# One sample of a streaming kernel is loaded as two halves, the second on four DMA engines

## Chip, core and metric

The kernel runs on one core of a Trainium2 chip. The metric is device time in microseconds (us), as the median of several executions. Times inside an execution come from one execution taken by the hardware profiler; they are counted from the start of its span, which is a little shorter than the execution's own time.

## What is computed

`x` is 128 samples of 128 x 1024 floats (512 KB each, 64 MB in all), `weights` holds eight 128 x 128 matrices, and `subjects` (the input `itok_B_0_7`) gives each sample the number of its matrix. Every sample is multiplied by its own matrix and added to the product:

```
B, C, D, T, N_SUBJECTS = (128, 128, 128, 1024, 8)
w = weights[subjects]
out = jnp.einsum('bct,bcd->bdt', x, w)
return x + out
```

All of `x` has to be read from HBM and all of the result, another 64 MB, written back.

## The kernel before

The samples go through in 32 groups of four (G = 2 samples in a pair, H = 2 pairs in a group, `NT` = 32). A group `i` lives in one of 12 SBUF slots, `xs[i % 12]`, each 128 partitions x 4 samples x 1024 floats. The result overwrites the sample in its slot and is stored from there.

Four sequences run side by side and meet in semaphores:

- **SP issues all loads**, in order of the samples (the loop at line 162). Each load is one DMA of 512 KB with a completion of 16 on the semaphore of its pair, `s_pair[slot][pair]`. Its HBM side is written as 32 rows of 16 KB (`ROWS` = 4 rows of `x` put together), its SBUF side as 128 partitions of 4 KB; spread over 16 DMA engines this is two pieces of 16 KB for each engine. The first 48 loads fill the 12 slots without a wait; from group 12 on, SP first waits until the store that empties the slot has landed (lines 164 to 167).
- **POOL copies the matrix** of each sample from `w_all` to one of four small buffers (line 196). Ahead of the first copy of a pair it waits that the PSUM buffer is free (`s_added`), and the copy itself carries the wait for the two loads of its pair (`loaded(i, q0)`).
- **PE and DVE** follow: two matmuls of 512 columns for each sample (line 206), then one addition over the pair (line 217).
- **ACT issues the stores**, one of 2 MB for each group, smaller ones for the first and the last group. The very last sample has a store of its own at line 231.

The semaphore arithmetic matters for the change: `s_pair` counts 16 for each load of the pair and 16 for the store of the group, and `loaded` and `emptied` give the counts to wait for. The function `transfer` (line 50) builds the DMA instruction with its access patterns as they are written, so the shapes of the two sides reach the queue unmerged.

Of the kernel before, what the change touches and what calls it, by code (L numbers as in the profile page):

```python
# [30 lines left out]
G = 2  # L31
H = 2
# [3 lines left out]
SLOTS = 12  # L36
# [5 lines left out]
DMA = 16  # L42

IDLE = 3

ROWS = 4
QUEUES = {mybir.EngineType.SP: "qSPDynamicHW", mybir.EngineType.Activation: "qActDynamicHW"}


def transfer(nc, engine, out, in_):  # L50

    later, nc._always_lower_symbolic_ap = nc._always_lower_symbolic_ap, False
    ins, outs = engine.lower_ap_dma(in_), engine.lower_ap_dma(out)
    nc._always_lower_symbolic_ap = later
    return engine.add_instruction(  # L57
        mybir.InstDMACopy(
            name=nc.get_next_instruction_name(),
            engine=engine.engine,  # L60
            ins=ins,
            outs=outs,
            mode="Copy",
            cce_op=ALU.bypass,
            queue=QUEUES[engine.engine],
        )
    )


@with_exitstack  # L70
def kernel(
    ctx: ExitStack,
    tc: tile.TileContext,
    x: bass.AP,
    subjects: bass.AP,
    weights: bass.AP,
    out: bass.AP,
):
    nc = tc.nc
    B, C, T = x.shape  # L80
    S, _, D = weights.shape
    NT = B // (G * H)

    def sbuf(name, *shape, dtype=F32):
        return ctx.enter_context(nc.sbuf_tensor(name, list(shape), dtype)).ap()

    given, near, wrap, index = (
        sbuf(name, 1, B, dtype=I32) for name in ("given", "near", "wrap", "index")
    )
    w_all = sbuf("w_all", C, S, D)  # L90
    ws = [sbuf(f"w{i}", C, 1, D) for i in range(W_SLOTS)]
    zeros = sbuf("zeros", C, N)
    xs = [sbuf(f"x{i}", C, H * G, T) for i in range(SLOTS)]
    ps = [
        ctx.enter_context(nc.psum_tensor(f"ps{i}", [D, G, T], F32)).ap() for i in range(P_SLOTS)
    ]

    s_given = tc.alloc_semaphore("s_given")
    s_wall = tc.alloc_semaphore("s_wall")
    s_index = tc.alloc_semaphore("s_index")  # L100
    s_zeros = tc.alloc_semaphore("s_zeros")
    s_copied = tc.alloc_semaphore("s_copied")
    s_product = tc.alloc_semaphore("s_product")
    s_added = tc.alloc_semaphore("s_added")

    s_pair = [[tc.alloc_semaphore(f"s_pair{i}_{h}") for h in range(H)] for i in range(SLOTS)]


    s_first = tc.alloc_semaphore("s_first")

    def emptied(i, h):

        turns = i // SLOTS
        return (DMA * G + (DMA if h == H - 1 else 0)) * turns

    def loaded(i, q):

        h = q // G
        return s_pair[i % SLOTS][h], emptied(i, h) + DMA * G

    def load(engine, i, q):
        k, h = i % SLOTS, q // G
        transfer(
            nc,
            engine,
            xs[k][:, q, :],
            x[i * H * G + q].rearrange("(a r) t -> a (r t)", r=ROWS),
        ).then_inc(s_pair[k][h], DMA)

    def store(i, q0, q1):  # L130
        k, b = i % SLOTS, i * H * G
        transfer(
            nc,
            nc.scalar,
            out[b + q0 : b + q1].rearrange("g d t -> d g t"),
            xs[k][:, q0:q1, :].rearrange("d (o g) t -> d o (g t)", g=min(G, q1 - q0)),
        ).then_inc(s_first if i == 0 and q1 == G else s_pair[k][(q1 - 1) // G], DMA)

    with tc.tile_critical():  # L139

        nc.scalar.dma_start(given, subjects.rearrange("(o b) -> o b", o=1)).then_inc(s_given, DMA)

        nc.vector.memset(zeros, 0.0).then_inc(s_zeros, 1)  # L143
        nc.tensor.wait_ge(s_zeros, 1)
        for _ in range(IDLE):
            nc.tensor.matmul(  # L146
                ps[P_SLOTS - 1][:, G - 1, :N], zeros[:, :D], zeros, start=True, stop=True
            )

        nc.vector.wait_ge(s_given, DMA)
        nc.vector.tensor_scalar(near, given, -S, S - 1, ALU.max, ALU.min).then_inc(s_index, 1)  # L153
        nc.vector.wait_ge(s_index, 1)
        nc.vector.tensor_scalar(wrap, near, 0, S, ALU.is_lt, ALU.mult).then_inc(s_index, 1)  # L155
        nc.vector.wait_ge(s_index, 2)
        nc.vector.tensor_tensor(index, near, wrap, ALU.add).then_inc(s_index, 1)  # L157
        nc.gpsimd.wait_ge(s_index, 3)


        nc.sync.dma_start(w_all, weights.rearrange("s c d -> c s d")).then_inc(s_wall, DMA)  # L161
        for i in range(NT):
            k = i % SLOTS
            if i == SLOTS:
                nc.sync.wait_ge(s_first, DMA)
            if i >= SLOTS:
                nc.sync.wait_ge(s_pair[k][H - 1], emptied(i, H - 1))
            for q in range(H * G):
                load(nc.sync, i, q)


        for j in range(NT * H):
            i, q0, q1 = j // H, j % H * G, (j % H + 1) * G
            k = i % SLOTS
            p = ps[j % P_SLOTS]

            ahead = j < P_SLOTS
            if ahead:  # L180
                nc.tensor.wait_ge(*loaded(i, q0))
            for q in range(q0, q1):
                b = i * H * G + q
                if b % R == 0:
                    _, subject = nc.values_load_multi_w_load_instructions(
                        index[0:1, b : b + R],
                        engines=[mybir.EngineType.Pool],
                        min_val=0,
                        max_val=S - 1,
                        skip_runtime_bounds_check_because="the index is clamped on the chip above",  # L190
                    )
                if b == 0:
                    nc.gpsimd.wait_ge(s_wall, DMA)
                if not ahead and q == q0:
                    nc.gpsimd.wait_ge(s_added, j - P_SLOTS + 1)
                copy = nc.gpsimd.tensor_copy(  # L196
                    ws[b % W_SLOTS], w_all[:, bass.ds(subject[b % R], 1), :]
                )
                if not ahead and q == q0:
                    copy.wait_op(*loaded(i, q0), "sem-ge")  # L200
            copy.then_inc(s_copied, 1)

            nc.tensor.wait_ge(s_copied, j + 1)
            for q in range(q0, q1):
                for t in range(0, T, N):
                    mm = nc.tensor.matmul(  # L206
                        p[:, q % G, t : t + N],
                        ws[(i * H * G + q) % W_SLOTS][:, 0, :],
                        xs[k][:, q, t : t + N],
                        start=True,  # L210
                        stop=True,
                    )
            mm.then_inc(s_product, 1)

            mine = xs[k][:, q0:q1, :]
            nc.vector.wait_ge(s_product, j + 1)
            nc.vector.tensor_tensor(  # L217
                mine, p, mine, ALU.add
            ).then_inc(s_added, 1)

            if i == 0 or q1 == H * G or i == NT - 1:
                nc.scalar.wait_ge(s_added, j + 1)
                store(i, q0 if i in (0, NT - 1) else 0, q1 - (b == B - 1))

    with tc.tile_critical() as waits:
        for i in range(NT - SLOTS, NT):
            nc.sync.wait_ge(s_pair[i % SLOTS][H - 1], emptied(i + SLOTS, H - 1))
        nc.sync.wait_ge(s_pair[(NT - 1) % SLOTS][0], emptied(NT - 1 + SLOTS, 0) + DMA)  # L230
    last = nc.scalar.dma_start(out[B - 1], xs[(NT - 1) % SLOTS][:, H * G - 1, :])

    tc.add_manual_dep(
        last.ins,
        waits.name,
        mybir.DependencyInfo(mybir.DependencyClass.NoSync, mybir.DependencyReason.SCHED_ONLY),
        reason="the end of the program waits for it",
    )
# [27 lines left out]
```

## Time and profile before

| what | value |
|---|---|
| median of 3 runs | 326.78 us (326.64 to 326.98) |
| the profiled execution | 327.18 us |
| its span | 325.4 us |
| data moved | 134.85 MB: 67.63 MB read from HBM, 67.11 MB written |
| packets of the loads' queue (q1, issued by SP) | 7184 |
| packets of the stores' queue (q10, issued by ACT) | 8882 |
| last matmuls and last addition end | 278.7 us |
| last store issued | 305.0 us |
| granted TensorE clock, mean | 0.924 |

How to read it: the compute engines are done some 46 us before the end. What is left in that time are stores that had been queued. The profile counts the share of time that the core's 16 DMA engines were moving packets; a share of 0.06 is one engine of 16. A few packets are neither loads nor stores: eight in the span are instruction fetches (four of 16 KB on queue q8, four of 8 KB on q14).

A DMA's completion is posted in 16 parts, one by each DMA engine after its own last piece. The trace has the time of each posting, though not the number of the engine.

### The profile page before, as it was taken

To read this page: it belongs to the slowest core of one execution; us is meant where nothing else is said; L and a number is where in the kernel's file an instruction comes from. 1 tells how busy PE (TensorE), PEld (TensorE's weight loads), DVE (VectorE), ACT (ScalarE), POOL (GpSimd) and SP (SyncE) were. 2 spreads that over 40 slices of the span, in tenths; PEclk is the share of its full clock that TensorE was granted. 3 is DMA by queue.
4 is the path that set the end of the run, shared out by engine and by line. 5 is a ranking of instruction groups with operands and counts; after the bars stand their busy time and mean duration, and the time that the engine had idled before them with its cause. 6 is when DMAs were issued, how large, how long until landed. Compare 5 with 4: busy or idle time off the path is not lost.

```text
span 325.4 us, 1606 instructions
## 1 busy us (share of the span) xinstructions
PE 241.1 (74%) x518; PEld 95.2 (29%) x518; DVE 147.9 (45%) x68; POOL 34.3 (11%) x132
## 2 busy tenths in 40 slices
PE   6999988988888888888888888888888689000000
PEld 2444332333333333333333333333333233000000
DVE  1375754555555555454555555554554544200000
POOL 1011111011111111111011111111111010000000
PEclk9999999999999999999999999999999889655555
DMA  6999999999999999999999999999999999999994
GB/s 250 413 418 421 428 425 422 420 428 427 426 421 427 429 415 427 424 431 423 423 435 417 416 432 424 428 417 428 433 419 424 418 437 415 429 425 427 426 428 201
DMA packets 16074, 134.85 MB, mean 414 GB/s; under 512 B 2625, under 2 KB 3650, under 8 KB 3906
## 3 DMA queue, kind: packets, MB, share of 16 engines
q1 hardware_dynamic: 7184, 67.64, 49.7%
q10 hardware_dynamic: 8882, 67.11, 49.1%
q8 instruction: 4, 0.07, 0.1%
q14 instruction: 4, 0.03, 0.0%
HBM read 67.63 MB, written 67.11 MB: 414 GB/s over the span
## 4 chain that ended last, share of the span: by engine, by line
PE 42%; DVE 20%; issue 16%; POOL 4%; DMA 2%; POOLq 1%; SPq 0%
PE ps L206 42%; DVE x L217 20%; POOL w L196 4%; DMA x<-in_x_dram 2%; POOLq L196 1%; SPq L57 0%; SPq L161 0%; POOLq L139 0%; SPq L262 0%; SPq L139 0%
## 5 line engine op out<-in xcount | busy, mean ns | idle before, releaser
L206 PE MATMUL ps<-x,w 128*128 128x512 f32 x512 | 236.1, 607 | 33.6 <-POOL w L196 32.1
L217 DVE TENSOR_TENSOR x<-ps,x 128x2048 f32<-128x2048 f32 x64 | 146.7, 2292 | 129.1 <-PE ps L206 129.1
L206 PEld LDWEIGHTS ps<-x,w 128*128 128x128 f32 x512 | 93.3, 191 | 176.6 <-issue 93.9
L196 POOL COPY w<-w_all 128x128 f32 x128 | 34.1, 296 | 238.0 <-DMA x<-in_x_dram 207.7
L146 PE MATMUL ps<-zeros 128*128 128x512 f32 x6 | 5.0, 992 | 1.7 <-DVE zeros L143 1.7
L146 PEld LDWEIGHTS ps<-zeros 128*128 128x128 f32 x6 | 1.8, 328 | 3.7 <-issue 2.1
L143 DVE MEMSET zeros<- 128x512 f32 x1 | 0.5, 485 | 1.1 <-SPq L139 1.1
L153 DVE TENSOR_SCALAR near<-given 1x128 int32<-1x128 int32 x1 | 0.2, 215 | 0.6 <-DMA given<-in_itok_B_dram 0.6
L157 DVE CUSTOM_DVE_ANT_0 index<-near,wrap 1x256 uint16<-1x256 uint16 x1 | 0.3, 278 | 0.0
L155 DVE TENSOR_SCALAR wrap<-near 1x128 int32<-1x128 int32 x1 | 0.2, 216 | 0.0
L253 POOL MEMSET const-float32-0.0<- 128x1 f32 x1 | 0.1, 99 | 0.2 <-issue 0.2
L253 POOL MEMSET const-bfloat16-1.0<- 128x1 bf16 x1 | 0.1, 102 | 0.0
L253 POOL MEMSET const-uint8-127<- 128x1 uint8 x1 | 0.1, 102 | 0.0
L253 POOL MEMSET const-float32-1.0<- 128x1 f32 x1 | 0.1, 99 | 0.0
## 6 DMA issues: line engine op xcount, KB each, us to landing
x<-in_x_dram SPq DMA_DIRECT2D x128, 512.0 KB, 32.3
out_dram<-x ACTq DMA_DIRECT2D x30, 2048.0 KB, 47.3
out_dram<-x ACTq DMA_DIRECT2D x3, 1024.0 KB, 13.9
out_dram<-x ACTq DMA_DIRECT2D x2, 512.0 KB, 21.1
w_all<-in_L_cond_weights_dram SPq DMA_DIRECT2D x1, 512.0 KB, 4.5
given<-in_itok_B_dram ACTq DMA_DIRECT2D x1, 0.5 KB
```

The costliest lines, as they stand in the source:

```text
L143: nc.vector.memset(zeros, 0.0).then_inc(s_zeros, 1)
L146: nc.tensor.matmul(ps[P_SLOTS - 1][:, G - 1, :N], zeros[:, :D], zeros, start=True, stop=True)
L153: nc.vector.tensor_scalar(near, given, -S, S - 1, ALU.max, ALU.min).then_inc(s_index, 1)
L155: nc.vector.tensor_scalar(wrap, near, 0, S, ALU.is_lt, ALU.mult).then_inc(s_index, 1)
L157: nc.vector.tensor_tensor(index, near, wrap, ALU.add).then_inc(s_index, 1)
L196: copy = nc.gpsimd.tensor_copy(ws[b % W_SLOTS], w_all[:, bass.ds(subject[b % R], 1), :])
L206: mm = nc.tensor.matmul(p[:, q % G, t : t + N], ws[(i * H * G + q) % W_SLOTS][:, 0, :], xs[k][:, q, t : t + N], start=True, stop=True,)
L217: nc.vector.tensor_tensor(mine, p, mine, ALU.add).then_inc(s_added, 1)
L253: nc = _bacc.Bacc("TRN2", target_bir_lowering=False, num_devices=1)
```

## The change

Sample 40 of 0 to 127 (the 41st; the first of group 10, in slot 10) is loaded by `load_apart` instead of `load`. Partitions 0 to 63 come in one DMA of 16 rows of 16 KB, one row for each of 16 engines, and count on a new semaphore `s_apart`. Partitions 64 to 127 come in a second DMA. Its HBM side is written with an outermost dimension of 4, each with 4 rows of 16 KB; it counts on the pair's semaphore, as the whole load did. By the change's own description these are four pieces for each of the first four engines. POOL waits for `s_apart` ahead of the copy for this sample.

The engines' instruction orders differ in nothing else: SP's 41st load is two DMA instructions in place of one, and POOL has one more wait.

```diff
+APART = 40
+FEW = 4
...
+    s_apart = tc.alloc_semaphore("s_apart")
...
+    def load_apart(engine, i, q):
+
+        k, h = i % SLOTS, q // G
+        half = C // 2
+        rows = x[i * H * G + q]
+        transfer(
+            nc,
+            engine,
+            xs[k][:half, q, :],
+            rows[:half].rearrange("(a r) t -> a (r t)", r=ROWS),
+        ).then_inc(s_apart, DMA)
+        transfer(
+            nc,
+            engine,
+            xs[k][half:, q : q + 1, :],
+            rows[half:].rearrange("(e a r) t -> e a (r t)", r=ROWS, e=FEW),
+        ).then_inc(s_pair[k][h], DMA)
...
             for q in range(H * G):
-                load(nc.sync, i, q)
+                (load_apart if i * H * G + q == APART else load)(nc.sync, i, q)
...
+                if b == APART:
+                    nc.gpsimd.wait_ge(s_apart, DMA)
                 copy = nc.gpsimd.tensor_copy(
```

## The prediction

> **What bounds the kernel now.** I read the DMA parts of the page first, because the compute engines end long before the span does. Rows of the page:
>
> ```profile
> DMA  6999999999999999999999999999999999999994
> ...
> q1 hardware_dynamic: 7184, 67.64, 49.7%
> q10 hardware_dynamic: 8882, 67.11, 49.1%
> q8 instruction: 4, 0.07, 0.1%
> q14 instruction: 4, 0.03, 0.0%
> ```
>
> Loads and stores together fill 98.8% of the time of 16 DMA engines: 321.5 of 325.4 us. The missing 3.9 us are the first two (nothing issued yet), the last one (nothing left), and the stretch in which the engines stop one after the other. The view of windows shows a middle stretch and that end; columns: window, length, busy time of four engines, PE clock, DMA share, GB/s:
>
> ```profile
> 60.00:120.00 60.00, 52.62 (x114) 20.12 (x112) 32.19 (x15) 7.89 (x30) 1.00 1.01 425
> ...
> 275.00:318.00 43.00, 1.35 (x4) 0.28 (x2) 2.29 (x1) 0.00 (x0) 0.55 1.01 426
> 320.00:320.50 0.50, 0.00 (x0) 0.00 (x0) 0.00 (x0) 0.00 (x0) 0.50 0.96 393
> 320.50:321.00 0.50, 0.00 (x0) 0.00 (x0) 0.00 (x0) 0.00 (x0) 0.50 0.57 229
> 321.00:321.50 0.50, 0.00 (x0) 0.00 (x0) 0.00 (x0) 0.00 (x0) 0.50 0.42 172
> 321.50:322.00 0.50, 0.00 (x0) 0.00 (x0) 0.00 (x0) 0.00 (x0) 0.50 0.30 123
> 322.00:323.00 1.00, 0.00 (x0) 0.00 (x0) 0.00 (x0) 0.00 (x0) 0.50 0.06 25
> 323.00:324.00 1.00, 0.00 (x0) 0.00 (x0) 0.00 (x0) 0.00 (x0) 0.50 0.06 25
> ```
>
> The reader is to see three things. All 16 engines are busy until 320.5 us. Then they drop out in a group (0.96 to 0.42) and a second group (0.30 to 0.06). From 322 to 324 us one engine of 16 works alone, at 25 GB/s, about what it had among 16 (425 / 16 = 26.6). So an engine has a pace of its own, and the kernel ends when the engine with most left to do ends. The trace's postings for the very last store say the same to 0.01 us; relative to the last of the 16:
>
> ```
> -3.78 -3.57 -3.48 -3.42 -3.37 -3.32 -3.29 -3.24 -3.03
> -2.39 -2.36 -2.19 -2.15 -2.13 -1.87
>  0.00
> ```
>
> Nine engines end 3.0 to 3.8 us early, six 1.9 to 2.4, and one is the laggard. The eight instruction fetches explain the six: one costs its engine 0.6 to 1.5 us. The laggard got one as well, but most of its lag grows evenly from 22 to 272 us, while loads run; in the store-only tail its packets take 311 ns, as the others' do.
>
> **What the change does to the sum.** From the windows' row, 16,384 B at 26.6 GB/s is 0.617 us for a piece; the pieces' own records say 0.616, and each starts 4 ns before its predecessor ends: 0.61 us. Before, each engine had two pieces of sample 40. After, engines outside the first four have one, the first four 1 + 4 = 5.
>
> - Twelve engines: 1 piece less, -0.61 us.
> - First four: 3 pieces more, 3 x 0.61 = +1.84 us, and one more posting (a 4 B packet of 9 ns).
>
> The bytes stay the same. What decides is where in the list of postings the first four stand, which the trace does not tell, as it gives no engine's number. The bounds are these. If the laggard is outside the four, it ends 0.61 us earlier. The four end at their old place + 1.84: engines of the nine at -3.03 + 1.84 = -1.19 or earlier, never last; engines of the six at -2.39 + 1.84 = -0.55 up to -1.87 + 1.84 = -0.03. So the end moves by -0.61 to -0.03. If the laggard is one of the four, it moves by +1.84.
>
> I take the laggard as outside. Counted over 16 engines the chance is 12 in 16. A row speaks for more: in the load-only stage (8 to 18 us) the 16 postings of each load come in one fixed order within 0.73 us, with one engine 0.12 us ahead of the rest, and the laggard at or next to the end of that order. If pieces are handed out by engine number, the laggard has a high one. Of the six, four would be spread over 15 engines, so that at least one probably lies among the first four; the engine at the head of that fixed order later takes two of the small fetches, and ends at about -2.36. That is the one I lean on: -2.36 + 1.84 = -0.52. With the middle of the six (-2.15) it would be -0.31. I take -0.45, nearer the first.
>
> A rule against this stands in the Trainium skill (DMA: Bandwidth & Descriptors, "Rules for kernel authors"): a small outermost dimension confines a DMA to as many engines, so use all 16. Taken alone it would price the change at the four engines' extra pieces, +1.84 us. The tail above disagrees in so far as 15 of 16 engines idle 1.9 us or more at the end; whether the four are of those no row shows. The same page ("Latency and other measured facts") calls engines 7 and 15 usually slower than the others, which would put the laggard outside the four; this trace has one such engine, not two, and no number on it.
>
> **What is late, and what hides it.** In 60 to 120 us the loads' queue has 58.8% of the engines' time, so a piece passes every 0.617 / 0.588 = 1.05 us on that queue. Three more pieces ahead make sample 40, and all loads behind it, land up to 3.1 us later on the four. The wait falls on POOL:
>
> ```profile
> L196 POOL COPY w<-w_all 128x128 f32 x128 | 34.1, 296 | 238.0 <-DMA x<-in_x_dram 207.7
> ```
>
> POOL already waits for loads (207.7 us over 55 waits), so its copies for sample 40 and everything behind them, the matmuls and the addition of that pair and the store of group 10, start up to 3.1 us later. That costs nothing: stores in this stretch take a median 51.8 us from issue to landing, so a store issued 3.1 us later still finds work queued ahead of it on every engine. Without that cover the price is 3.1 us, 329.9. The new wait for `s_apart` is met earlier than the one on the copy behind it, since the first half goes ahead on the same queue; its own price is a sequencer piece of 0.05 us. SP issues one DMA more:
>
> ```profile
> x<-in_x_dram SPq DMA_DIRECT2D x128, 512.0 KB, 32.3
> ```
>
> One issue takes SP 0.47 us at the least and 1.2 at the median. The 87 loads behind it move by that, with 32.3 us between issue and landing to hide it. Uncovered it is 0.5 to 1.2 us. The slots freed later wait for the slowest engine's stores; engines ahead of it spend that time on queued stores, so they lose nothing.
>
> Sum: against the profiled 327.18 us, -0.45, so 326.73; the runs' median lies 0.40 lower, and 326.78 - 0.45 = 326.33. I write 326.3.
>
> **The rivals.** *The laggard is among the first four.* It gets the three pieces, and the end moves by +1.84: 328.6 us, slower. It decides as soon as any of the four stood later than -1.84 in the list; the laggard alone does. For it: 4 engines of 16. Against it: its place in the fixed order.
>
> *The lag belongs to the recording.* It grows while instructions run, and the profiled execution is 0.40 us longer than the median. If without a profile the laggard were no later than the six, the six would set the end at -1.87 now. After, four of the nine would end at -3.03 + 1.84 = -1.19, which is 0.68 later; one of the six would be up to 1.84 later: 327.5 to 328.6. Against it: a lag of 1.87 that came from the recording would make the profiled time longer by more than the 0.40.
>
> *The second half isn't confined to four engines.* If it were spread over 16 engines, each would keep two pieces: 326.8, no change. For it: nothing in the profile before shows a load with such a shape. Against it: a rank of 4 outermost rows can't be dealt evenly to 16. The skill's page (section "Why a DMA increments its semaphore by 16 and not by 1") takes the largest number up to 16 that divides both sides' outermost sizes, here 64 and 4, and the lowest-numbered engines; no run here shows it yet.
>
> **How the numbers follow.** A measurement of this kernel tells about 0.2% (0.65 us) from no change. Forecast 0.70: 326.17 to 326.75 from the bounds, 326.0 with half the 0.34 us spread of the runs. Its better end lies just at the limit: I give 0.28 of it to more than 0.65 us gained, 0.42 to within. Laggard among the four 0.13; lag of the recording 0.11; no confinement 0.06. So faster 0.28, same 0.42 + 0.06 = 0.48, slower 0.13 + 0.11 = 0.24. The range 326.0 to 327.5 holds the forecast, the third rival and the low edge of the second, about 0.8. The likeliest case alone is 326.0 to 326.8.
>
> **What would show it.** The queue q1 should have 7188 packets: 20 postings for the two halves where there were 16. In the last store's postings, twelve should stand where they were against the start, less 0.61 us, and four 1.84 us later; the lone stretch (share 0.06) should shrink from 2 us to 0.1 to 1.3 us. A lone stretch of four engines (0.25) for over a microsecond, or an end later than 324.4 us, would make the prediction wrong; so would DMA shares under 0.98 between 90 and 270 us, as cover that failed.

## The result and the profile after

The changed kernel takes 328.26 us (median of 6 runs, 327.81 to 328.63) where the kernel before takes 326.69 us in the same comparison (6 runs, 326.08 to 326.98). The ratio is 1.0051, with a 95% interval of 1.0041 to 1.0062: slower by half a per cent, about 1.6 us. The forecast was 326.3, its range ended at 327.5.

The profiled execution took 328.63 us, with a span of 326.9. Rows of its page, the DMA share in 40 slices of 8.17 us, what the engines moved in each slice, and the loads' queue:

```profile
DMA  7999999999999999999999999999999999999994
GB/s 247 417 410 426 430 428 424 415 428 415 358 426 431 421 417 428 426 427 422 424 430 427 419 419 431 424 420 427 426 428 420 430 427 418 424 428 425 427 428 202
...
q1 hardware_dynamic: 7188, 67.64, 49.8%
```

Two things are to be seen. The queue has the 7188 packets that the two halves should give. And one slice, the eleventh (81.7 to 89.9 us), moved 358 GB/s where its neighbours moved 415 to 426, while the row of shares above it shows nothing: a share counts the time in which packets were under way, so packets that take longer keep it full. The view of windows over that stretch (window, length, busy time of PE, weight loads, DVE and POOL, PE clock, DMA share, GB/s), first before, then after:

```profile
80.00:82.00 2.00, 1.98 (x5) 0.57 (x3) 0.00 (x0) 0.31 (x2) 1.00 0.96 406
82.00:84.00 2.00, 1.72 (x4) 0.87 (x5) 1.98 (x1) 0.23 (x1) 1.00 1.01 426
84.00:86.00 2.00, 1.98 (x5) 0.57 (x3) 0.31 (x1) 0.00 (x1) 1.00 1.02 430
86.00:88.00 2.00, 1.41 (x4) 0.70 (x5) 1.98 (x1) 0.53 (x2) 1.00 1.04 438
```

```profile
80.00:82.00 2.00, 1.90 (x5) 0.57 (x3) 0.07 (x1) 0.25 (x2) 1.00 1.06 360
82.00:84.00 2.00, 1.66 (x4) 0.87 (x5) 2.00 (x1) 0.28 (x2) 1.00 0.96 299
84.00:86.00 2.00, 2.00 (x5) 0.57 (x3) 0.23 (x1) 0.00 (x0) 1.00 1.03 356
86.00:88.00 2.00, 0.04 (x1) 0.00 (x0) 1.93 (x1) 0.00 (x0) 1.00 0.95 373
```

In the 8 us in which sample 40 passes, the engines moved 299 to 373 GB/s in place of 406 to 438. In the packet records of that stretch, three quarters of the 16 KB loads take 640 to 1070 ns instead of 616, and almost half of the 8 KB stores 340 to 640 instead of 311. I call this the dip. From here on its size is read from one window, 78 to 90 us, against the usual 425 GB/s:

```profile
78.00:90.00 12.00, 10.81 (x24) 4.31 (x24) 6.58 (x3) 1.29 (x5) 1.00 1.01 424
```

```profile
78.00:90.00 12.00, 7.40 (x16) 2.88 (x16) 6.51 (x3) 1.04 (x5) 0.97 1.01 374
```

Before, nothing is lost. After, (425 - 374) / 425 x 12 us = 1.44 us, and since it is the mean over 16 engines, all of them end later by about that. The packet records give the same: what packets in that window took beyond 616 and 311 ns, summed and divided by 16, is 1.48 us after and 0.01 before. This second measure is the sharper one, since windows of 12 us elsewhere in the kernel before move 419 to 431 GB/s, which is 0.2 us either way. PE drops from 24 matmuls to 16 in the window (the pair with sample 40 is late, as the prediction had it); that was hidden, as from 90 to 270 us the engines moved 425 GB/s both before and after.

The rows of POOL's copies and of the loads' issues (count, KB each, median us to landing), on which the cover of the late loads rested, changed little but for the split load (before: 207.7 us of waiting for loads, 32.3 us to landing):

```profile
L221 POOL COPY w<-w_all 128x128 f32 x128 | 33.8, 293 | 240.6 <-DMA x<-in_x_dram 202.2
...
x<-in_x_dram SPq DMA_DIRECT2D x127, 512.0 KB, 30.0
...
x<-in_x_dram SPq DMA_DIRECT2D x2, 256.0 KB, 34.4
```

The end of the changed kernel, in windows:

```profile
321.00:322.00 1.00, 0.00 (x0) 0.00 (x0) 0.00 (x0) 0.00 (x0) 0.50 0.73 299
322.00:323.00 1.00, 0.00 (x0) 0.00 (x0) 0.00 (x0) 0.00 (x0) 0.50 0.52 213
323.00:324.00 1.00, 0.00 (x0) 0.00 (x0) 0.00 (x0) 0.00 (x0) 0.50 0.32 131
324.00:325.00 1.00, 0.00 (x0) 0.00 (x0) 0.00 (x0) 0.00 (x0) 0.50 0.10 41
325.00:326.00 1.00, 0.00 (x0) 0.00 (x0) 0.00 (x0) 0.00 (x0) 0.50 0.03 12
```

The engines now drop out over 4.3 us, with less of a step between the groups; the last one is alone for about a microsecond, up to 325.5. To see who it is, the packet records can be sorted into 16 chains: on one engine a packet starts 4 ns before its predecessor ends, and every engine has the same known sequence of pieces. (The sorting is my reading; the trace names no engine, and two engines in step can be swapped.) The four that got five pieces are recognised by the loads they still have ahead of them at 92 us, the laggard by the 1.8 to 2.4 us that its packets lose, spread over the time after 100 us. Their ends in us from the start of the span:

```
               first four                          laggard    clean ones of the rest
before         (not told apart)                    324.00     320.3 to 321.0
after          323.88 323.99 324.54 325.53         324.23     321.2 to 321.9
```

The laggard is not among the four. The last engine is one of the four, one that also takes small instruction fetches. And the dip is everyone's: the clean engines of the rest have a piece less (0.6 us) and still end 0.9 us later than before, which makes 1.5 us.

### The profile page after: what moved, and what is told of

Its sections match the earlier page's. It is cut to its first block, busy times and chain, and to the rows that moved or that the text cites. A ratio compares the mean times of both kernels' runs of the same rounds, so it can differ in the third digit from the quotient of the medians.

```text
span 326.9 us, 1608 instructions
## 1 busy us (share of the span) xinstructions
PE 242.2 (74%) x518; PEld 95.8 (29%) x518; DVE 147.9 (45%) x68; POOL 34.0 (10%) x132
## 3 DMA queue, kind: packets, MB, share of 16 engines
q1 hardware_dynamic: 7188, 67.64, 49.8%
## 4 chain that ended last, share of the span: by engine, by line
PE 43%; DVE 19%; issue 17%; POOL 4%; DMA 2%; POOLq 1%; SPq 0%
PE ps L231 43%; DVE x L242 19%; POOL w L221 4%; DMA x<-in_x_dram 2%; POOLq L221 1%; POOLq L208 0%; SPq L60 0%; SPq L184 0%; POOLq L162 0%; SPq L287 0%; SPq L162 0%
```

## The experiments

Two theories of the dip were tried first: that halves of 64 partitions make it (the half-partition theory), or that confining 256 KB to four engines makes it (the confinement theory). Each kernel below changes only the body of `load_apart`, unless said.

**Halves, no confinement.** Both halves on 16 engines.

```diff
-            xs[k][half:, q : q + 1, :],
-            rows[half:].rearrange("(e a r) t -> e a (r t)", r=ROWS, e=FEW),
+            xs[k][half:, q, :],
+            rows[half:].rearrange("(a r) t -> a (r t)", r=ROWS),
```

> Sample 40 in two halves of 64 partitions, both dealt to all 16 DMA engines: the confinement to four is undone, the halves stay. If the halves themselves make the dip (64 partitions reach too little of SBUF at a time), the stretch of 80 to 88 us moves less than 400 GB/s again, every engine loses 1.2 to 1.5 us, and the time is about 328.0 us. If the dip comes from four engines with a large share each, there is no dip, each engine has its two pieces as before, and the time is 326.7 us.

Measured 327.03 us against 326.62 (ratio 1.0012, 1.0003 to 1.0022). The window:

```profile
78.00:90.00 12.00, 9.98 (x22) 4.12 (x23) 6.51 (x3) 1.20 (x5) 1.00 1.01 411
```

A dip, but of 14 / 425 x 12 = 0.40 us (0.46 by the packet records), some quarter of the whole. Both expectations miss: halves cost something, and not most of it.

**Confinement, no halves.** One DMA for all of sample 40, 128 partitions, on the first four engines; no second DMA and no `s_apart`.

```diff
...
+            xs[k][:, q : q + 1, :],
+            rows.rearrange("(e a r) t -> e a (r t)", r=ROWS, e=FEW),
...
```

> Sample 40 as one load over 128 partitions, all of it on the first four engines: 6 pieces more for each of the four (3.7 us), 2 less for twelve. No halves. If halves of the partitions make the dip, there is none, and the four engines end at -2.4 + 3.7 = +1.3 us against the old end: about 328.0 us, with a stretch of four engines at the end. If confinement makes the dip, it is twice as long as with half a sample, and the time is 330 to 331 us.

Measured 331.43 us (ratio 1.0144, 1.0127 to 1.0161), above both expectations.

```profile
78.00:90.00 12.00, 6.75 (x16) 2.46 (x14) 5.65 (x3) 0.53 (x2) 0.99 1.01 382
```

A dip of 1.21 us without any half. So confinement with 16 KB pieces makes a dip too, though not a longer one for eight pieces than for four. By the chains the four end at 325.37, 325.72, 326.79 and 328.19, and no other engine after 323.2: the four are a fixed set, the laggard isn't in it (it ends at 323.17).

**The same bytes for each engine, split by columns.** Halves of 512 columns, each over all 128 partitions; the second on four engines or on eight. A piece is 2 KB now.

```diff
+        half = T // 2
+        rows = x[i * H * G + q]
+        transfer(nc, engine, xs[k][:, q, :half], rows[:, :half]).then_inc(s_apart, DMA)
...
+            xs[k][:, q : q + 1, half:],
+            rows[:, half:].rearrange("(e a) t -> e a t", e=FEW),
...
```

For eight engines, `e=8` stands in place of `e=FEW`.

> Sample 40 in two halves of 512 columns, each over all 128 partitions; the first on 16 engines, the second on four. The bytes per engine are those of the changed kernel (32 KB less on nobody, 48 KB more on four, 16 KB less on twelve). If halves of the partitions make the dip, it is gone, and the ledger of the prediction holds: 326.2 to 326.7 us. If four engines with a large share make it, the dip stays, 327.5 to 328.3 us.

> As the split by columns, but the second half on eight engines: they get 16 KB more each, the other eight 16 KB less. If the laggard is outside the first eight and there is no dip: it ends 0.61 us earlier and the engines with fetches at -1.87 + 0.61, so 326.1 us. If the laggard is among the first eight: 327.3 us. With a dip from confinement: 0.5 to 1 us more than these.

On four engines 326.79 us against 326.62 (1.0004, 0.9994 to 1.0013), just above the 326.2 to 326.7 of the ledger, and no dip:

```profile
78.00:90.00 12.00, 6.89 (x16) 2.58 (x14) 5.79 (x3) 0.53 (x2) 0.99 1.02 427
```

This is the changed kernel without its dip: same bytes on the same four engines. The chains give the prediction's ledger to look at:

```
               first four                          laggard    clean ones of the rest
by columns     322.23 322.33 323.68 323.84         322.60     319.6 to 320.3
```

On eight engines 327.27 us (1.0016, 1.0006 to 1.0026), no dip either (425 GB/s in the window), and one engine alone at the end:

```profile
322.00:323.00 1.00, 0.00 (x0) 0.00 (x0) 0.00 (x0) 0.00 (x0) 0.50 0.12 49
323.00:324.00 1.00, 0.00 (x0) 0.00 (x0) 0.00 (x0) 0.00 (x0) 0.50 0.07 29
324.00:325.00 1.00, 0.00 (x0) 0.00 (x0) 0.00 (x0) 0.00 (x0) 0.50 0.03 12
```

By the chains it is the laggard, at 324.61, with the extra pieces of the eight. As it isn't in the first four, the laggard is one of the second four engines. And neither theory of the dip stands as it was: four confined engines make no dip when their pieces are small.

**Where the halves land.** Same HBM reads in the same pieces, but to the even and the odd partitions in place of the lower and the upper half; first with both halves on 16 engines, then with the second on four. The diff is against the plain halves on 16 engines. In these two kernels and the next, the rows of sample 40 come to lie in another order than the kernel is asked for; bytes and pieces are the same.

```diff
-            xs[k][:half, q, :],
+            xs[k][0:C:2, q, :],
...
-            xs[k][half:, q, :],
+            xs[k][1:C:2, q, :],
```

> The two halves on 16 engines, reading the same HBM rows in the same pieces, but the first half goes to the even partitions and the second to the odd ones, so each half spans all 128 partitions (the rows of sample 40 stand in another order, so its output differs). If the dip of 0.45 us an engine in the plain halves came from writing into one half of SBUF's partitions, it falls to under 0.15 us and the stretch of 80 to 84 us moves 415 GB/s or more. If it came from the HBM side or from there being two DMAs, it stays at 0.45 us and 373 GB/s.

> The changed kernel with the first half written to the even partitions and the second, on four engines, to the odd ones; HBM reads as in the changed kernel (rows of sample 40 in another order). If the SBUF side makes the dip: the first part of it (0.73 us an engine before 83 us) mostly goes, to under 0.4 us; the second part (0.75 us) shrinks too, as each of the four engines now moves over twice as many partitions for a piece; 327.0 to 327.6 us. If the HBM side makes it, both parts stay, 328.2 us.

On 16 engines 326.83 us against 326.64 (1.0006, 0.9996 to 1.0016), on four 327.67 (1.0033, 1.0020 to 1.0045):

```profile
78.00:90.00 12.00, 10.01 (x23) 3.88 (x22) 5.79 (x4) 1.59 (x6) 1.00 1.01 420
```

```profile
78.00:90.00 12.00, 8.36 (x18) 3.32 (x18) 6.08 (x3) 1.06 (x4) 0.93 1.01 398
```

0.14 us in place of 0.40 (by the packet records 0.22 in place of 0.46), and 0.76 in place of 1.44. Nothing changed but the partitions written, so that side makes about half of the dip. The rest is more than was expected: on 16 engines the stretch of 80 to 84 us moved 406 GB/s, not 415. In the packet records of the kernel with four engines, the loss after 83 us fell from 0.75 to 0.22 us and the one before only from 0.74 to 0.60, where under 0.4 was expected: a part of the first stays without a cause that I can name.

**Where the reads come from.** SBUF targets as in the changed kernel; the four engines read interleaved rows.

```diff
-            rows[half:].rearrange("(e a r) t -> e a (r t)", r=ROWS, e=FEW),
+            rows[half:].rearrange("(a e r) t -> e a (r t)", r=ROWS, e=FEW),
```

> The changed kernel with SBUF targets as they were, but each of the four engines reads rows 64 KB apart and its neighbour reads the row beside it, where before each engine read 64 KB in one run (rows of sample 40 in another order). If the SBUF side makes the dip, nothing changes: 328.2 us, 1.4 to 1.5 us lost by every engine. If four engines at a pitch of 64 KB collide in HBM, the second part of the dip goes: 327.4 us.

328.35 us (1.0049, 1.0032 to 1.0065).

```profile
78.00:90.00 12.00, 7.40 (x16) 2.88 (x16) 6.71 (x3) 1.38 (x6) 0.99 1.01 380
```

A dip of 1.27 us. That is 0.17 under the changed kernel's, less than that kernel's own two profiles differ (below). So the order in which the four engines read HBM is not the cause.

**How fast they are written.** The four engines' pieces are cut to 4 KB; bytes, rows and partitions stay.

```diff
-            rows[half:].rearrange("(e a r) t -> e a (r t)", r=ROWS, e=FEW),
+            rows[half:].rearrange("(e a) t -> e a t", e=FEW),
```

> The changed kernel with the second half cut into 4 KB pieces, 16 for each of the four engines in place of four of 16 KB. Bytes and targets stay. Queues take turns by the piece, so the loads of the four engines then have about a third of their engines' time beside 8 KB pieces of stores, where they had two thirds. If the dip comes from the pace at which four engines write foreign partitions, the second part shrinks to under 0.3 us, 327.3 to 327.7 us; if it comes from the targets as such, it stays, only longer drawn out, 328.2 us.

327.27 us (1.0018, 1.0009 to 1.0028).

```profile
78.00:90.00 12.00, 7.40 (x16) 2.88 (x16) 6.43 (x3) 0.62 (x3) 0.98 1.01 399
```

The dip is 0.73 us, half of the changed kernel's, with 0.35 us of it after 83 us by the packet records: more than the 0.3 expected, half of the 0.75 before. The size of the pieces matters, and with it the pace; with the same targets a dip stays at 4 KB too.

**The small parts by themselves, a second profile, and a version meant to be faster.** The split by columns with both halves on 16 engines has every added instruction and moves nothing between engines; the changed kernel is profiled again; and the second half is cut to 384 columns, on the four engines (the diff is against the split by columns on four).

```diff
-        half = T // 2
+        half = 640
```

> Sample 40 in two halves of 512 columns over all partitions, both on 16 engines: the second DMA, its issue on SP, the new semaphore and POOL's wait are there, but no bytes move between engines and no DMA is confined. If those parts cost nothing, as the prediction had it, the time is that of the kernel before, 326.6 us, within 0.2 us. If the added issue or wait costs, 327.1 us or more.

> The changed kernel once more, for a second profile. If the dip belongs to the change, the stretch of 80 to 88 us moves about 350 GB/s again and every engine loses 1.4 to 1.5 us in it; if it was an accident of one execution, the stretch moves 415 GB/s or more.

> A version meant to be faster: sample 40 split by columns, 640 on 16 engines and 384 on the first four. Twelve engines, the laggard with them, move 12 KB less (0.46 us), the four 36 KB more (1.38 us). By the ledger the laggard ends 0.46 us earlier and the two of the four with fetches at -2.1 to -1.9 + 1.4 = -0.5 to -0.7 us, so 326.2 us, 0.14% less than before. If splitting costs the engines more than it shows, 326.6 us or more.

The first takes 326.48 us against 326.80 (0.9991, 0.9982 to 1.0001): the second DMA, its issue, the semaphore and POOL's wait cost nothing that this comparison can tell. The second profile of the changed kernel (one execution, 329.04 us) shows the dip again, (425 - 366) / 425 x 12 = 1.67 us:

```profile
78.00:90.00 12.00, 7.46 (x17) 2.87 (x16) 6.87 (x3) 1.07 (x4) 1.00 1.00 366
```

By the chains its four end at 323.87, 324.06, 325.71 and 325.92 and the laggard at 324.44, so there too the last engine is one of the four.

The split at 640 columns takes 326.48 us against 326.80, ratio 0.9987 (0.9978 to 0.9996). It is faster than the kernel before by 0.13% (0.14% was expected), about as much as such a comparison can tell; its interval overlaps that of the split with both halves on 16 engines, so it isn't shown that the moved bytes bring it. By the chains the four end at 321.62, 322.30, 323.17 and 323.35 and the laggard at 322.56, which is the order that the ledger gives.

## Why the prediction was wrong

**The step that failed** is the price of a moved piece: "First four: 3 pieces more, 3 x 0.61 = +1.84 us", and "the bytes stay the same". It counts a piece as 0.61 us of its own engine and of nobody else's. That came from "an engine has a pace of its own", read from the end of the kernel, where only stores run, and carried over to loads of another shape. In its place the runs showed 1.44 us lost by all 16 engines while the pieces pass. The split by columns, which gives each engine the same bytes without the dip, lies 0.17 us above its kernel before; the changed kernel lies 1.57 us above its own. The 1.4 us between them is the dip. The term of the sum for it was zero, and no rival had it; the rival that came near the measured time, the laggard among the four, is refuted by the chains. The second rival, a lag of the recording, holds the measured time in its 327.5 to 328.6, but asks for 0.7 us or more from the same bytes by columns, where 0.17 was measured. The third is refuted by the 7188 packets, four postings more than before.

**What makes it** is shown in part. Two things matter, each changed alone. One is the partitions written: even and odd ones in place of a lower and an upper half take the dip from 1.44 to 0.76 us, and from 0.40 to 0.14 with 16 engines. The other is the size of the four engines' pieces: 4 KB in place of 16 KB leave 0.73. Another order of the HBM rows leaves 1.27. The partitions alone don't decide: all of sample 40 on four engines and the half by columns on four engines both give each of the four 32 neighbouring partitions, and the first, with 16 KB pieces, has a dip of 1.21 us, the second, with 2 KB pieces and half of the bytes, none. Whether one cause lies behind both is not shown. The Trainium skill (SBUF — State Buffer, "Door 1: The DMA port swizzle") states that DMA reaches SBUF over 16 ports, that the lower 64 partitions lie on eight of them and the upper 64 on the other eight, and puts the limit for 64 partitions at half of that for 128. That is a rule against this change that I hadn't weighed. The runs agree in direction, as by that page's map the even partitions, and the odd ones, reach all ports. But the load of all 128 partitions on four engines dips as well; no run shows a port, and a dip that slows all 16 engines about alike isn't what one or two crowded ports would give by themselves. How the wait spreads to every engine stays open.

**Point by point for the rest.**

- The moved pieces: right. By columns, the clean engines outside the four end at a mean of 320.0 us where before it was 320.6, -0.6; the two of the four without late fetches end 2.26 us after those (322.28 in the mean), where 4 pieces of 0.61 make 2.44. So the term was right where nothing dips.
- The laggard outside the four: right. That it lies late in the order of numbers: not borne out, it is among the second four of 16. So what held was the count, 12 in 16, and not the reason that was to raise it.
- Which of the four would set the end: right in kind. I leaned on the engine with two small fetches at -2.36 + 1.84 = -0.52; two of the four take fetches and end at 323.68 and 323.84 by columns, 0.2 to 0.3 above 323.5.
- The size of the gain: off even without the dip, +0.04% where -0.14% was forecast. The laggard ended at 324.00 in the profile before, but at 323.15 in the split by columns on 16 engines, which has the same bytes for each engine. The profiled execution was 0.4 us above the median, and I took its lag for the usual one. So the laggard's lead is probably a second term that was mis-sized: -0.45 was forecast, and the split by columns measured +0.17, which is 0.6 us; the dip makes the rest of the +1.57.
- Late loads and their cover, the added DMA, the added wait: right, as the split by columns on 16 engines and the 425 GB/s after 90 us show.
- The sign that I named for failing cover, a DMA share under 0.98, would also have been the wrong gauge for the dip: between 80 and 88 us it stayed at 0.95 to 1.06, while GB/s fell by up to 30%. The sign that did come true is the end after 324.4 us.

A residue: in the changed kernel the last engine ends 0.6 us later than before + 1.84 + 1.44 gives (325.53 to 324.95), and with all of sample 40 on four engines 1.6 us later. By the chains that engine loses 2.1 us in the changed kernel's dip, where the mean is 1.4; why, no run tells.

## What to carry to other kernels

When transfers are moved between DMA engines, price the time of everyone else's packets too: here the pieces' SBUF partitions and size decided whether the move was free. What was free here was to give few engines more work by splitting along the free axis, in 2 KB pieces over all partitions; a half of the partitions in 16 KB pieces was not. And look for contention in GB/s or in packet durations, since busy shares stay full.

## What the hardware showed unexpectedly

- On a DMA engine the two queues took turns by single pieces, though of unequal size: in the split by columns on four engines, 2 KB loads took 84 ns each, but the last of them started at 94.5 us where the first did at 78.4, as on the four engines an 8 KB store of 311 ns stood between one and the next.
- One DMA engine of 16, among the second four, is slower than the others while loads run (1.8 to 2.4 us lost after 100 us, most of it a few ns a packet; the others 0.1 us, apart from waits for fetches), and not in the store-only end. Which of those four it is, no run tells. The Trainium skill (DMA: Bandwidth & Descriptors, "Latency and other measured facts") calls engines 7 and 15 usually slower and, as a best guess, ties that to transfers issued from GpSimd; here all are issued by SP and ACT, and only one engine lags.
